# The last two projections taken apart into seven block products each, worked in pairs of batches

## The chip, the cores and the metric

One core of one Trainium2 chip runs the whole program. The time is device time in microseconds (us), the median of several executions. The program streams 128 batches through one long loop, so the steady turn of the loop, two ticks for four batches in the terms used below, repeated some 30 times, decides almost everything; the start and the drain are a few per cent.

## The reference, cut to what matters

```python
# layer 0: attention with a mask that multiplies the scores
h = jnp.maximum(_layernorm(x), 0.0)
q, k, v = (proj(Wq, bq), proj(Wk, bk), proj(Wv, bv))         # 512 x 512 each, 8 heads of 64
scores = einsum('bhqd,bhkd->bhqk', q, k) * SCALE * (adj + adj)[:, None]
ctx = einsum('bhqk,bhkd->bhqd', softmax(scores), v)
x = x + einsum('bse,fe->bsf', ctx, Wo) + bo                  # the output projection
# layer 1: graph attention
h = jnp.maximum(_layernorm(x), 0.0)
Wh = einsum('bsi,io->bso', h, W)                             # layer 1's projection
e = leaky_relu(Wh @ a[:512] + swapaxes(Wh @ a[512:], 1, 2), 0.2)
att = softmax(where(adj > 0.5, e, -9e15), axis=1)
x = x + elu(einsum('bst,bto->bso', att, Wh))
```

All is float32; x is 128 batches of 128 rows by 512 columns.

## The kernel before

The projections to q, k and v already use seven block products in place of eight (a "unit" below is one such product of a group of four batches: eight matmul instructions of 256 columns). The output projection and layer 1's projection are plain: four accumulating matmuls of 512 columns per batch, each into a PSUM tile of 512 columns, called a bank here.

```python
    def rows_matmul(lhsT, w):
        pm = ps1.tile([P, E], F32, name="pm", tag="ps1")
        for c in range(C):
            nc.tensor.matmul(pm, lhsT[:, c, :], w[:, c, :], start=(c == 0), stop=(c == C - 1))
        return pm

    def output0(b):
        po = rows_matmul(cxs[b], wo_sb)
        nc.vector.tensor_tensor(xs[b], po, xs[b], OP.add)
        l1s[b] = row_stats(xs[b])

    def hidden1(b):
        mv, rstd = l1s[b]
        h2 = work.tile([P, E], F32, name="h2", bufs=3)
        nc.vector.tensor_scalar(h2, xs[b], mv[:, 0:1], 0.0, op0=OP.subtract, op1=OP.max)
        # ... two dot products with u_src and u_dst on VectorE
        nc.vector.tensor_scalar(neg, adjTs[b], 0.5, NEG_INF, op0=OP.is_le, op1=OP.mult)

    def scores1(b):
        # ... broadcast transpose into pb, then
        nc.scalar.activation(w, pb, AF.Prelu, bias=ws[:, 1:2], alpha=ALPHA)
        nc.vector.tensor_tensor(w, w, neg, OP.add)
        nc.vector.tensor_reduce(nmx, w, AX.X, OP.max, negate=True)
```

One tick of its loop handles one batch t of attention, batch t-1 of the output projection and batch t-2 of layer 1 (the issue of loads, the drain and some helpers cut):

```python
            scores1(t - 2); softmax1(t - 2)
            scores(t); mask(t)
            done = unit(0); scale1(t - 2); done()
            exps(t); hidden(...); normalise(t)
            output0(t - 1)
            unit(1)()
            hidden1(t - 1)
            unit(2)()
            gather1(t - 2)
            done = unit(3); hidden(...); done()
            attn_T(t)
            unit(4)()
            stats0(far + 3); shift(t)
            output1(t - 2)
            unit(5)()
            context(t)
```

## Time and profile before

| | before |
|---|---|
| median time | 2660.1 us (2659.26 to 2661.6, 3 runs) |
| TensorE busy | 2615.8 us, 98% |
| VectorE / ScalarE busy | 1830 us, 69% / 1151 us, 43% |
| mean granted clock of TensorE | 0.997 |
| four batches in the steady loop | 81.14 us (40.57 a pair) |

TensorE is packed: instructions follow each other without gaps in the loop (2513.2 us busy of the 2521 between 79 and 2600 us), at full clock (1.00 in that stretch).

### The profile page before, as it was taken

What the parts mean: (1) busy time and instruction counts of PE and PEld (TensorE: products, weight loads), DVE (VectorE), ACT (ScalarE), POOL (GpSimd) and SP (SyncE); (2) the same over time, 40 slices, a digit from 0 to 9 for tenths busy, and PEclk for the clock granted to TensorE, in tenths of its full rate; (3) what the DMA queues carried; (4) which work ended last, traced back from release to release, by engine and by line L of the source; (5) the groups of instructions that cost most, each with busy time, mean ns of one, the idle gap of its engine ahead of it and who ended that gap; (6) DMA issues with size and microseconds to landing.
All of it is one profiled execution on the core that took longest, in us unless ns stands there. A gap on an engine that the chain in (4) does not pass through costs nothing.

```text
span 2655.8 us, 38303 instructions
## 1 busy us (share of the span) xinstructions
PE 2615.8 (98%) x13744; PEld 1882.8 (71%) x13744; DVE 1830.3 (69%) x3509; ACT 1151.3 (43%) x3595; POOL 334.7 (13%) x647
## 2 busy tenths in 40 slices
PE   7999999999999999999999999999999999999996
PEld 6677777777777777777777777777777777777763
DVE  5776767766676767677666767676776667676655
ACT  2444444444444444444444444444444444444443
POOL 1111111111111111111111111111111111111001
PEclk9999999999999999999999999999999999999999
DMA  4433322222321232222222223322222232122010
GB/s 153 68 74 70 64 64 64 65 64 66 77 56 57 74 70 64 64 65 63 64 67 77 58 54 75 69 64 64 66 62 64 67 77 58 55 75 57 31 40 20
DMA packets 209133, 173.29 MB, mean 65 GB/s; under 512 B 48432, under 2 KB 158000, under 8 KB 208560
## 3 DMA queue, kind: packets, MB, share of 16 engines
q1 hardware_dynamic: 207360, 170.84, 26.2%
q8 instruction: 109, 1.79, 0.4%
q14 instruction: 80, 0.66, 0.1%
q10 hardware_dynamic: 1584, 0.01, 0.0%
HBM read 137.11 MB, written 33.68 MB: 64 GB/s over the span
## 4 chain that ended last, share of the span: by engine, by line
PE 97%; DVE 2%; ACT 1%; DMA 1%; issue 0%; SPq 0%; ACTq 0%; DVEq 0%
PE pm L157 33%; PE acc_a L238 25%; PE acc_c L238 13%; PE acc_b L238 6%; PE sc L290 5%; PE pc L331 5%; PE pa L320 4%; PE pg L389 4%; PE pb L363 1%; ACT at L307 1%; DMA hT<-in_xT 0%; DVE at L314 0%; DVE nmx L300 0%; DVE at L296 0%; PE pt L177 0%; DMA x<-in_x 0%
## 5 line engine op out<-in xcount | busy, mean ns | idle before, releaser
L157 PE MATMUL pm<-w,gT 128*128 128x512 f32 x1024 | 464.0, 596 | 1.5 <-ACT gT L391 1.5
L157 PE MATMUL pm<-wo,cxT 128*128 128x512 f32 x1024 | 460.9, 593 | 0.5 <-ACT cxT L336 0.5
L307 ACT ACTIVATE at<-at,nmx 128x128 f32<-128x128 f32 x1024 | 395.6, 388 | 130.5 <-DVE nmx L300 130.5
L150 POOL TENSOR_SCALAR mv<-mv 128x1 f32<-128x1 f32 x256 | 117.1, 458 | 2149.8 <-DVE mv L147 2149.6
L157 PEld LDWEIGHTS pm<-w,gT 128*128 128x128 f32 x1024 | 195.4, 191 | 194.1 <-issue 185.9
L157 PEld LDWEIGHTS pm<-wo,cxT 128*128 128x128 f32 x1024 | 194.1, 190 | 191.1 <-issue 183.7
L399 DVE SCALAR_TENSOR_TENSOR x<-pm,x 128x512 f32<-128x512 f32 x128 | 88.5, 692 | 341.5 <-ACT ez L398 341.5
L398 ACT ACTIVATE ez<-pm 128x512 f32<-128x512 f32 x128 | 76.5, 598 | 399.2 <-PE pm L157 399.2
L238 PE MATMUL acc_a<-hT,wq 128*128 128x256 f32 x1024 | 246.7, 384 | 0.0
L238 PE MATMUL acc_a<-hT,wk 128*128 128x256 f32 x1024 | 245.3, 382 | 0.0
L238 PE MATMUL acc_a<-wv,hT 128*128 128x256 f32 x1024 | 244.2, 381 | 0.7 <-ACT v L250 0.7
L238 PEld LDWEIGHTS acc_a<-hT,wq 128*128 128x128 f32 x1024 | 190.7, 191 | 40.5 <-issue 14.8
L238 PEld LDWEIGHTS acc_a<-wv,hT 128*128 128x128 f32 x1024 | 189.4, 190 | 38.6 <-issue 14.8
L238 PEld LDWEIGHTS acc_a<-hT,wk 128*128 128x128 f32 x1024 | 187.2, 190 | 38.6 <-issue 14.8
L322 ACT COPY aT<-pa 128x1024 f32<-128x1024 f32 x128 | 129.6, 1012 | 147.4 <-PE pa L320 144.7
L307 ACT ACTIVATION_READ_ACCUMULATOR at<-at,nmx 128x1 f32 x1024 | 191.8, 187 | 0.0
L255 ACT ACTIVATE qT<-acc_a,bq 128x256 f32<-128x256 f32 x256 | 107.2, 470 | 194.6 <-PE acc_a L238 194.6
L145 DVE BATCH_NORM_STATS2 st<-x 128x6 f32<-128x512 f32 x256 | 176.4, 689 | 9.1 <-DMA x<-in_x 4.5
L151 POOL TENSOR_TENSOR mv<-mv,mhalf 128x1 f32<-128x1 f32 x256 | 177.3, 693 | 21.3
L331 PEld LDWEIGHTS pc<-aT,v 128*64 128x64 f32 x2048 | 109.2, 136 | 83.4 <-issue 83.4
L255 ACT ACTIVATE kT<-acc_a,bk 128x256 f32<-128x256 f32 x256 | 107.4, 471 | 134.0 <-PE acc_a L238 134.0
L314 DVE TENSOR_TENSOR at<-at,rs 128x1024 f32<-128x1024 f32 x128 | 156.8, 1225 | 4.4
(92 smaller groups left out, 3926.3 us busy)
## 6 DMA issues: line engine op xcount, KB each, us to landing
x<-in_x SPq DMA_DIRECT2D x256, 256.0 KB, 3.5
out<-x SPq DMA_DIRECT2D x128, 256.0 KB, 2.1
hT<-in_xT SPq DMA_DIRECT2D x120, 256.0 KB, 10.6
mr<-rows SPq DMA_DIRECT2D x120, 128.0 KB, 3.4
adj<-in_adj SPq DMA_DIRECT2D x128, 64.0 KB, 2.1
adjT<-in_adjT SPq DMA_DIRECT2D x128, 64.0 KB, 2.0
rows<-mv SPq DMA_DIRECT2D x120, 1.0 KB, 8.5
wq<-in_wqT SPq DMA_DIRECT2D x1, 1024.0 KB, 7.2
```

The lines of the kernel that those rows point to most:

```text
L145: nc.vector.bn_stats(st, src)
L150: nc.gpsimd.tensor_scalar_add(rstd, rstd, EPS)
L151: nc.gpsimd.tensor_tensor(rstd, rstd, mhalf, OP.pow)
L157: nc.tensor.matmul(pm, lhsT[:, c, :], w[:, c, :], start=(c == 0), stop=(c == C - 1))
L238: nc.tensor.matmul(acc[:, m, :], lhsT, rhs, start=fresh and m == 0 and c == 0, stop=c == 1, skip_group_check=True)
L255: nc.scalar.activation(dst(t, f)[:, m, :], a[:, m, :], AF.Identity, bias=bias[:, j : j + 1])
L290: nc.tensor.matmul(sc[:, s * C + i, :], qT[r, i, cols], kT[r, i, cols], start=True, stop=True)
L307: nc.scalar.activation(at[:, j, :], at[:, j, :], AF.Exp, bias=nmx[:, j : j + 1], accum_out=sums[:, j : j + 1])
L314: nc.vector.tensor_tensor(at, at, rs[:, :, None].to_broadcast([P, H, S]), OP.mult)
L320: nc.tensor.transpose(pa[:, j, :], at[:, j, :], ident)
L322: nc.scalar.copy(aT, pa)
L331: nc.tensor.matmul(pc[s * D : (s + 1) * D, i, :], vs[b // G][:, b % G, head * D : (head + 1) * D], ats[b][:, s * C + i, :], start=True, st ...
```

## The change

The intent is to take an eighth of the matmul work out of the last two projections too, by the scheme that q, k and v use already. Seven products of half-sized blocks need two batches as their two row blocks, so the pipeline goes by pairs: a tick is now a pair, with attention of batches a and b one after the other. VectorE gets the sums for the left factors and the adds of the products; to relieve it, layer 1's relu moves to ScalarE, and its mask is folded into one pass. The core of the diff, cut:

```diff
-    def rows_matmul(lhsT, w):
-        pm = ps1.tile([P, E], F32, name="pm", tag="ps1")
-        for c in range(C):
-            nc.tensor.matmul(pm, lhsT[:, c, :], w[:, c, :], start=(c == 0), stop=(c == C - 1))
-        return pm
+    PRODUCTS = [(0, 0, "a"), (1, 2, "b"), (5, 5, "a"), (6, 1, "c"), (4, 4, "a"), (2, 3, "a"), (3, 6, "c")]
+    def product_rows(left, w, which, n):
+        la, wb, bank = PRODUCTS[n]
+        slot = 1 if bank == "b" else 0
+        own = "c" if bank == "c" else "a"
+        if n == 0 or n == 3:
+            accs[which, own] = ps1.tile([P, 2, E // 2], F32, name="row_" + own, tag="ps1")
+        acc = accs[which, own][:, slot, :]
+        for c in range(2):
+            nc.tensor.matmul(
+                acc, left[:, la, c, :], w[:, wb, c, :], start=n in (0, 3) and c == 0, stop=c == 1, skip_group_check=True
+            )
+        return acc
     ... (output0: each product is added by VectorE as soon as it is there)
+        def done():
+            if n == 0 or n == 1:
+                add(0, 0, acc)
+            elif n == 2:
+                add(1, 0, acc)
     ...
-        nc.vector.tensor_scalar(h2, xs[b], mv[:, 0:1], 0.0, op0=OP.subtract, op1=OP.max)
+            nc.scalar.activation(h2[:, i, :], xs[p][:, i, :], AF.Relu, bias=nmr[:, i : i + 1], scale=mv[:, 1, i : i + 1])
     ...
+        nc.vector.scalar_tensor_tensor(w, adjTs.pop(p), 0.5, pb, op0=OP.is_le, op1=OP.subtract)
+        for i in range(2):
+            nc.scalar.activation(w[:, i, :], w[:, i, :], AF.Prelu, bias=ws[:, i, 1:2], scale=-MASK, alpha=ALPHA)
     ... (the tick, its first half; e is the pair in layer 1, o the one in the output projection, f the one that ends)
+            if attn:
+                scores(a)
+            if f is not None:
+                finish_a(f)
+            unit()()
+            if e is not None:
+                scores1(e)
+            if attn:
+                exps(a, range(4))
+            if e is not None:
+                softmax1(e)
+            if o is not None:
+                output0(o, 0)()
+            if attn:
+                exps(a, range(4, H))
+            if o is not None:
+                output0(o, 1)()
     ... (finish_b, a unit)
+            if e is not None:
+                scale1(e)
+            if attn:
+                normalise(a)
+            if o is not None:
+                output0(o, 2)()
     ... (unit, gather1, hidden, unit, attn_T(a), the first two products of output1, context(a), scores(b), ...)
     ... (the tick's end, its conditions cut: attn_T(b), hidden1(o), unit, output1(e, 5), then)
+            dots1(o, 0)
+            output1(e, 6)()
+            context(b)
+            dots1(o, 1)
+            elu(e)
+            context_sums()
```

Here o0, o1, o2 are the first products of `output0`; o0 and o1 take the two halves of one bank (`slot`). `scores(a)` also holds the VectorE work on the scores: the mask and its maximum.

## The prediction

> **What bounds the kernel now.** I read the page's busy shares first, then the chain that ended last, then the waits, then the timeline of one tick (one batch) in the steady part, then the stretches of the last 90 us.
>
> ```profile
> PE 2615.8 (98%) x13744; PEld 1882.8 (71%) x13744; DVE 1830.3 (69%) x3509; ACT 1151.3 (43%) x3595; POOL 334.7 (13%) x647
> PE 97%; DVE 2%; ACT 1%; DMA 1%; issue 0%; SPq 0%; ACTq 0%; DVEq 0%
> PE pm L157 33%; PE acc_a L238 25%; PE acc_c L238 13%; PE acc_b L238 6%; PE sc L290 5%; PE pc L331 5%; PE pa L320 4%; PE pg L389 4%; PE pb L363 1%; ACT at L307 1%; DMA hT<-in_xT 0%; DVE at L314 0%; DVE nmx L300 0%; DVE at L296 0%; PE pt L177 0%; DMA x<-in_x 0%
> ```
>
> TensorE is the chain (97%), and a third of it is pm, the output projection and layer 1's projection, the two that the change takes apart. A PE at 98% may still be loosely packed, so the starts matter more than the durations. From the chain in order of time, then the timeline of TensorE:
>
> ```profile
> 2453.30 3.45 PE acc_a L238 x16
> 2534.44 3.45 PE acc_a L238 x16
> ```
>
> ```profile
> 1212.81 3.60 PE L157 MATMUL pm<-wo,cxT 128*128 128x512 f32 x8
> 1216.24 1.89 PE L238 MATMUL acc_a<-hT,wq 128*128 128x256 f32 x8
> 1217.97 1.89 PE L238 MATMUL acc_b<-hT,wk 128*128 128x256 f32 x8
> 1219.69 1.05 PE L389 MATMUL pg<-w,h 128*128 128x128 f32 x8
> ```
>
> The same point of the loop returns after 81.14 us, for four batches: 40.57 us a pair. Eight instructions of 512 columns take 3.43 us from start to start, eight of 256 columns 1.73 us (0.216 each), so splitting columns costs nothing. No gap follows, because every input was ready long before. In this part VectorE and ScalarE never hold TensorE; the list of waits has TensorE waiting 18.3 us for normalised attention, six times, all at the end.
>
> The durations I need stand in the timeline of all engines, same tick:
>
> ```profile
> 1211.27 1.22 DVE L296 SCALAR_TENSOR_TENSOR at<-sc,adj 128x1024 f32<-128x1024 f32 x1
> 1212.52 1.22 DVE L300 TENSOR_REDUCE nmx<-at 128x8 f32<-128x1024 f32 x1
> 1213.65 0.15 DVE L380 RECIPROCAL rs<-sums 128x1 f32<-128x1 f32 x1
> 1213.77 0.40 ACT L307 ACTIVATE at<-at,nmx 128x128 f32<-128x128 f32 x1
> 1214.17 0.39 ACT L307 ACTIVATE at<-at,nmx 128x128 f32<-128x128 f32 x1
> 1222.32 1.04 PE L320 MATMUL pa<-ident,at 128*128 128x128 f32 x8
> 1223.39 1.01 ACT L322 COPY aT<-pa 128x1024 f32<-128x1024 f32 x1 [1.96 <-PE pa L320]
> ```
>
> A VectorE instruction of 1024 columns blocks the next for 1.25 us if that one needs its result, 1.13 if not. An exp of one head takes 0.39 us, four 1.55. ScalarE starts 0.2 us after TensorE has moved on.
>
> [...] The trace agrees: VectorE's order in the tick is the program's order. So one instruction that waits holds everything behind it. [...] The trace has 692 ns at 512 columns, 286 at 128[...]. So my estimate for the new 256-column operations is 0.42 us, blocking 0.45 or 0.34 us. [...] The trace, by stretches, after a wait of 3.0 us in the tail (columns from the second: length, PE, PEld, DVE, ACT, POOL, granted clock):
>
> ```profile
> 2603.00:2607.00 4.00, 0.97 (x9) 0.81 (x8) 1.69 (x3) 2.71 (x13) 0.00 (x0) 1.00 0.00 0
> 2607.00:2610.00 3.00, 3.00 (x11) 1.82 (x11) 2.83 (x7) 1.01 (x1) 1.50 (x2) 0.63 0.00 0
> 2610.00:2613.00 3.00, 3.00 (x6) 0.91 (x4) 1.02 (x4) 0.00 (x0) 0.62 (x1) 0.80 0.00 0
> ```
>
> It cost 1.7 us there (3 x 0.37 + 3 x 0.20), once in four waits of that length.
>
> **The change, part by part.** *TensorE work.* Removed per pair: 4 runs of pm, 4 x 3.43 = 13.72 us. Added: 14 products of 2 matmuls, each run as two instructions: 56 x 0.2156 = 12.07 us. Gain 1.65 us a pair, 38.9 us instead of 40.57; 64 x 1.65 = 106 us in all.
>
> *VectorE and ScalarE.* Added per pair: 8 sums of 256 columns for the left sides, 10 adds of 256 columns in place of 2 of 512. Removed: the relu of 0.48 x 2 (to ScalarE), the separate mask. Paired instructions save fixed cost. By the blocking times VectorE has some 32 us of work in 38.9. That is not a bound by itself, but it leaves little room for waits.
>
> *The order.* This is where I expect the change to lose. Take a tick (now a pair) with TensorE starting scores(a) at 0. TensorE's order is scores 1.15, projection unit 1.73, broadcast transposes 0.37, o0 and o1 (first two products of the output projection), so o1 would start at 0 + 1.15 + 1.73 + 0.37 + 0.86 = 4.1. But o0 and o1 are two halves of one PSUM bank, so o1 must wait until VectorE has added o0. In VectorE's order that add stands behind: the previous tick's last sums, mask(a) 1.25, its maximum 1.13, finish_a 1.13, the one-pass mask of layer 1 0.34, a round trip over ScalarE's Prelu 0.8, that maximum 0.35. With the add itself (0.45) this is 5.45 us after mask(a) starts.
>
> When does mask(a) start? At 1.35 at the earliest (scores ready). Before it VectorE must end the previous tick: attention's transpose ends at E-2.75 (E is the end of that tick's TensorE work: w5, w6 and context follow, 0.86 + 0.86 + 1.03), ScalarE copies it until E-1.55, only then comes the new relu (0.65, estimated from 598 ns for 512 columns plus a bias), so the first dot products start at E-0.9: dots 1.48, an add 0.35, dots 1.48, four sums 1.6: mask(a) at E+4.0. Where the previous tick is odd there is one more unit (1.73 us) behind the transpose; then the last dots end near E+1.35 and mask(a) is at E+2.9.
>
> So o0 is added at 2.9 + 5.45 = 8.4 (even ticks) and 4.05 + 5.45 = 9.5 (odd ticks), against 4.1: stalls of 4.3 and 5.4 us, mean 4.9. A second wait lies almost at the same depth in odd ticks: gather needs scale1, which stands behind q4's add, which waits for q4's copy on ScalarE behind all eight exps: 8.0 + 0.65 + 1.55 + 0.8 + 1.55 + 0.85 + 0.6 + 0.6 = 14.6; TensorE gets there at 9.3 + 5.4 = 14.7. It adds nothing once o1 has stalled, but would hold 5 us if o1 did not. The second half of the tick has slack: normalise(b) is due some 13 us after scores(b) and needs about 9.
>
> *Sum.* 38.9 + 4.9 = 43.8 us a pair, +3.2 on 40.57. For the 60 pairs of the full loop: +195 us. Clock: the idle stretches of 4.3 to 5.4 us exceed those that already dropped the clock; I take half the ticks at 1.2 us: +36. Start and tail: the first product waits behind sums of wv (some 3 us) and the last ticks are pair-long chains: +10. 2660 + 195 + 36 + 10 = 2901; I choose 2890.
>
> **Rivals.** (A) The stalls are hidden and TensorE stays packed: 2660 - 106 + 10 = about 2565. For it: the kernel before shows that such a schedule can be built. Against: even with mask(a) at 1.35, o0 is added at 6.8, 2.7 us late, and the gain is 1.65. (B) The compiler keeps the halves of the bank apart by address: o1 is free, and gather is the first wait, 1.9 us in even ticks (scale1 ends at 11.1 against 9.3) and 5.4 in odd ones: mean 3.6, (38.9 + 3.6 - 40.57) x 60 = +116, about 2790. (C) The previous tick's dots and sums overlap better than I think and mask(a) starts at 1.35 always: 2.7 us stall, +1.05 x 60 = +63, about 2735. (D) The clock drops in every tick: 2950. (E) VectorE becomes the bound: its 32 us plus waits of some 8 us would come near 43 anyway, so it can't be told from my own case by time alone; its busy share would be near 90%. (F) Transfers: the loads of the transposed x are issued a tick ahead and landed in 10.6 us; I expect none.
>
> **Range and chances.** C to D spans 2735 to 2950; with B between, I take 2740 to 2990 for 8 in 10. Faster needs both the bank wait and the tail chain to be wrong: 0.09. Within 2% (to 2713) needs stalls below 2.5 us a tick: 0.1. Slower: 0.81.
>
> **What would show it.** Right: TensorE's share falls to about 88 to 91%; the first in the list of TensorE's waits is the row accumulator on VectorE's add into x, 4 to 5 us some 60 times; VectorE 72 to 78%; granted clock below 9 tenths in some slices; the chain mixes DVE and ACT with PE. Wrong: PE still at 97% of the chain (A); waits chiefly at pg on w (B); a mask(a) that starts within 1.5 us of scores (C).

## The result and the profile after

| | before | after |
|---|---|---|
| median of the same rounds | 2659.95 us (4 runs, 2659.26 to 2661.6) | 3026.81 us (4 runs, 3026.47 to 3027.43) |
| TensorE busy | 2615.8 us | 2684.9 us |
| granted clock | 0.997 | 0.923 |
| four batches in the loop | 81.14 us | 92.16 us |

The change makes the kernel slower: ratio 1.1378, 95% interval 1.1359 to 1.1398. All ratios here are the mean time of one kernel's fast runs over the mean of the other's fast runs of the same rounds, so they are not quite the ratio of the medians quoted. The lower clock is in each of the four runs (0.923 or 0.924), so it belongs to the kernel.

From the page of the kernel after, busy time and then the chain that ended last, by engine and by line:

```profile
PE 2684.9 (89%) x15288; PEld 2265.9 (75%) x15288; DVE 2047.6 (68%) x3781; ACT 1301.2 (43%) x3915; POOL 119.1 (4%) x263
...
PE 73%; DVE 18%; issue 4%; ACT 4%; DMA 1%; POOL 0%; SPq 0%; POOLq 0%; DVEq 0%; ACTq 0%
PE acc_a L243 21%; PE row_a L295 17%; PE acc_c L243 9%; PE acc_b L243 7%; PE row_c L295 6%; DVE junk L407 6%; PE pg L445 4%; PE pa L334 4%; DVE at L312 3%; DVE x L490 3%; PE sc L310 2%; PE pc L354 2%; ACT w L421 1%; ACT aT L336 1%; DVE cxT L147 1%
```

Before, TensorE was 97% of the chain; now VectorE is 18% of it, by name the dot products (junk), the mask (at), the ending add (x L490) and the sums (cxT): instructions that stand ahead of o0's add. And TensorE is busy for longer than before with less to compute, which points to instructions that ran slower. The list of TensorE's waits (us in total, times, longest) begins with the one that was foretold:

```profile
PE row_a L295 <- DVE x L368: 296.4, 67, 8.7
```

In TensorE's timeline (start, length, instruction, instructions in the group; in brackets the recorded idle before it and who ended it) this is o0, o1 and the unit after them, in an even tick and then an odd one:

```profile
2539.41 1.03 PE L295 MATMUL row_a<-wo,cxT 128*128 128x256 f32 x4
2544.35 2.07 PE L295 MATMUL row_a<-wo,cxT 128*128 128x256 f32 x4 [3.91 <-DVE x L368]
2546.22 3.62 PE L243 MATMUL acc_b<-wv,hA 128*128 128x256 f32 x8
...
2584.69 1.03 PE L295 MATMUL row_a<-wo,cxT 128*128 128x256 f32 x4
2590.78 2.07 PE L295 MATMUL row_a<-wo,cxT 128*128 128x256 f32 x4 [5.06 <-DVE x L368]
2592.65 2.88 PE L243 MATMUL acc_a<-hS,wq 128*128 128x256 f32 x8
```

Two things are to be seen. First the wait: o1 stands 4.08 us behind where it could start in the even tick (2539.41 + 0.86 = 2540.27 to 2544.35), 5.23 us in the odd one. Second the lengths after it: o1 takes 2.07 us where o0, the same four instructions, took 1.03; the unit takes 3.62 or 2.88 instead of 1.89. The wait costs a second time, as clock.

What VectorE and ScalarE did in the odd tick's wait, from the timeline of all engines. TensorE's tick starts at 2581.55 with the scores of a:

```profile
2579.81 1.52 ACT L400 ACTIVATE h<-x,nmr,mv 128x512 f32<-128x512 f32 x2
2580.66 0.69 DVE L407 SCALAR_TENSOR_TENSOR junk<-h,u_src 128x512 f32<-128x512 f32 x1 [1.09 <-ACT h L400]
...
2583.69 0.42 DVE L146 TENSOR_TENSOR cxT<-cxT 128x256 f32<-128x256 f32 x1
...
2585.28 1.22 DVE L312 SCALAR_TENSOR_TENSOR at<-sc,adj 128x1024 f32<-128x1024 f32 x1
2586.53 1.22 DVE L316 TENSOR_REDUCE nmx<-at 128x8 f32<-128x1024 f32 x1
2587.67 1.22 DVE L490 SCALAR_TENSOR_TENSOR x<-z,x 128x1024 f32<-128x1024 f32 x1
2588.80 0.41 DVE L419 SCALAR_TENSOR_TENSOR w<-adjT,pb 128x256 f32<-128x256 f32 x1
2589.25 0.69 ACT L421 ACTIVATE w<-w,ws 128x128 f32<-128x128 f32 x2 [4.32 <-DVE w L419]
...
2590.31 0.41 DVE L368 TENSOR_TENSOR x<-row_a,x 128x256 f32<-128x256 f32 x1
```

The relu on ScalarE ends at 2581.33, 0.22 us before this tick begins, so most of the dot products and all sums of the previous pair run into this tick; the mask starts 3.73 us after the tick's start; and o0's add, the last line, ends 5.44 us after the mask started. o1 starts 0.06 us later. VectorE keeps the program's order here: o0 ends at 2585.72 (2584.69 + 1.03), but its add stays behind layer 1's maximum, which starts at 2589.98 after VectorE has sat idle for 0.76 us until ScalarE's Prelu is done.

The record of the granted clock changes in steps; I set the edges of the stretches on those steps (columns: stretch, length, PE, PEld, DVE, ACT, POOL, then granted clock, DMA share, GB/s):

```profile
2543.45:2550.28 6.83, 5.93 (x14) 4.71 (x15) 2.72 (x5) 3.91 (x21) 0.00 (x0) 0.50 0.19 74
...
2585.55:2587.82 2.27, 0.17 (x1) 0.00 (x0) 2.24 (x3) 0.00 (x0) 0.00 (x0) 1.00 0.00 0
2587.82:2594.65 6.83, 3.87 (x9) 3.12 (x10) 3.70 (x6) 4.54 (x22) 0.00 (x0) 0.50 0.00 1
```

The clock is halved for 6.83 us in either tick, and TensorE works for 5.93 and 3.87 us of it. Work at half clock takes twice as long (2.07 us for o1 against o0's 1.03), so half of that time is lost: (5.93 + 3.87) / 2 = 4.90 us in two ticks.

### The profile page after: what moved, and what is told of

Read it like the earlier page. It is cut to its first block, busy times and chain, and to the rows that moved or that the text cites. A ratio compares the mean times of both kernels' runs of the same rounds, so it can differ in the third digit from the quotient of the medians.

```text
span 3025.7 us, 40583 instructions
## 1 busy us (share of the span) xinstructions
PE 2684.9 (89%) x15288; PEld 2265.9 (75%) x15288; DVE 2047.6 (68%) x3781; ACT 1301.2 (43%) x3915; POOL 119.1 (4%) x263
## 3 DMA queue, kind: packets, MB, share of 16 engines
q8 instruction: 120, 1.97, 0.3%
## 4 chain that ended last, share of the span: by engine, by line
PE 73%; DVE 18%; issue 4%; ACT 4%; DMA 1%; POOL 0%; SPq 0%; POOLq 0%; DVEq 0%; ACTq 0%
PE acc_a L243 21%; PE row_a L295 17%; PE acc_c L243 9%; PE acc_b L243 7%; PE row_c L295 6%; DVE junk L407 6%; PE pg L445 4%; PE pa L334 4%; DVE at L312 3%; DVE x L490 3%; PE sc L310 2%; PE pc L354 2%; ACT w L421 1%; ACT aT L336 1%; DVE cxT L147 1%
## 5 line engine op out<-in xcount | busy, mean ns | idle before, releaser
L295 PE MATMUL row_a<-wo,cxT 128*128 128x256 f32 x1280 | 408.3, 449 | 296.7 <-DVE x L368 296.4
L295 PEld LDWEIGHTS row_a<-wo,cxT 128*128 128x128 f32 x1280 | 277.6, 227 | 366.0 <-DVE x L368 325.3
L295 PE MATMUL row_a<-w,gT 128*128 128x256 f32 x1280 | 330.2, 381 | 3.5 <-ACT z L466 1.9
L368 DVE TENSOR_TENSOR x<-row_a,x 128x256 f32<-128x256 f32 x320 | 134.5, 420 | 219.0 <-PE row_a L295 216.0
L295 PEld LDWEIGHTS row_a<-w,gT 128*128 128x128 f32 x1280 | 235.8, 191 | 34.2 <-ACT z L466 3.7
L312 DVE SCALAR_TENSOR_TENSOR at<-sc,adj 128x1024 f32<-128x1024 f32 x128 | 156.2, 1221 | 67.5 <-PE sc L310 67.5
L316 DVE TENSOR_REDUCE nmx<-at 128x8 f32<-128x1024 f32 x128 | 156.1, 1220 | 4.4
L243 PE MATMUL acc_a<-hS,wq 128*128 128x256 f32 x512 | 151.7, 450 | 0.0
L310 PE MATMUL sc<-kT,qT 64*128 64x128 f32 x2048 | 149.6, 286 | 0.0
L354 PE MATMUL pc<-aT,v 128*64 128x128 f32 x2048 | 141.0, 280 | 1.1 <-ACT aT L336 1.1
```

The lines of the kernel that those rows point to most:

```text
L243: nc.tensor.matmul(acc[:, m, :], lhsT, rhs, start=fresh and m == 0 and c == 0, stop=c == 1, skip_group_check=True)
L295: nc.tensor.matmul(acc, left[:, la, c, :], w[:, wb, c, :], start=n in (0, 3) and c == 0, stop=c == 1, skip_group_check=True)
L310: nc.tensor.matmul(sc[:, s * C + j, :], qT[r, j, cols], kT[r, j, cols], start=True, stop=True)
L312: nc.vector.scalar_tensor_tensor(at, sc, QSCALE, adjs[p][:, i : i + 1, :].to_broadcast([P, H, S]), op0=OP.mult, op1=OP.mult)
L316: nc.vector.tensor_reduce(nmx, at, AX.X, OP.max, negate=True)
L354: nc.tensor.matmul(pc[s * D : (s + 1) * D, j, :], vs[b // G][:, b % G, head * D : (head + 1) * D], aT[:, s * C + j, :], start=True, stop=True,
```

## The experiments

The theory has three parts. The bank: o1 waits only because it shares a bank with o0. The queue: the add that it waits for is late by VectorE's order, not by VectorE's load. The clock: each of these waits halves the clock for a while, which the prediction had put far too low. Rivals: VectorE is simply full (the prediction's E); and the halved clock is no effect of the waits, or costs only as much as predicted, and the rest is work in the loop that the sums missed. All seven kernels computed correct results. Six of them ran once; the kernel before took 2660.96 us (median of 7, from 2657.65 to 2664.73) beside the first four of them, 2662.61 and 2660.02 us beside the later ones. So runs of one kernel spread over some 7 us, and differences in total time that are read from single runs below are 66 us or more; the run with one useless matmul is read from the length of its turns instead.

### The second product in a bank of its own

```diff
-        slot = 1 if bank == "b" else 0
-        own = "c" if bank == "c" else "a"
-        if n == 0 or n == 3:
+        slot = 0
+        own = bank
+        if n == 0 or n == 1 or n == 3:
```

(and `start=n in (0, 1, 3)`.) It does so in both projections.

> The second product of each row projection gets a PSUM bank of its own. Mine: the changed kernel's wait at o1 (4.1 and 5.2 us in even and odd ticks) is one of the shared bank; with its own bank o1 runs at once, and TensorE waits later and in pieces: at o2 for the add of o0 (1.4 and 2.5 us), then in odd ticks at pg for w (2.4 us). Stalls 1.4 and 4.9 a tick, no piece over 3 us, so the clock seldom drops: 2740 to 2800 us, granted clock over 0.96. Rival (o1 waits for something else, such as the data of x or the queue): no change, 3010 to 3040.

Measured: 2809.38 us, clock 0.973, against 3026.81. The first two of TensorE's waits, and an odd tick:

```profile
PE row_a L295 <- DVE x L368: 131.7, 64, 5.6
PE pg L445 <- DVE rs L327: 27.9, 30, 2.3
```

```profile
2404.21 1.16 PE L295 MATMUL row_a<-wo,cxT 128*128 128x256 f32 x4 [2.47 <-DVE x L368]
```

The line is o2: it accumulates onto o0, so it has to wait for the same add, but one product and one unit (2.6 us) later. o1 no longer waits at all. The second line of the list is the gather's wait that rival B foresaw; it comes in odd ticks only, 0.9 us in the mean where B, which had no wait of o2 before it, had 5.4. So it was the sharing that held o1. The edit gives o1 a tile of its own and with it another place in PSUM, and which of the two the program's wait goes by, this run can't tell. The next waits in line are what the change would have cost without it: 2.47 us in odd ticks, 1.32 in even ones. The time lies 9 us above the expected range. The clock record says why: 33 spells of one window of 3.41 us each at half clock, of which TensorE works 3.30 us in the mean, 33 x 3.30 / 2 = 54 us. At full clock it would be some 2755 us, an estimate from that record.

### The ending add behind o0's add instead of ahead of it

```diff
-            if f is not None:
-                finish_a(f)
             unit()()
     ...
             if o is not None:
                 output0(o, 0)()
+            if f is not None:
+                finish_a(f)
```

> One VectorE instruction of 1.13 us (finish_a) goes from before the one-pass mask to after the add of o0; nothing else changes. Mine: the wait at o1 shrinks by 1.13 us in every tick (to about 3.0 and 4.1), 70 us in all, and the clock, which drops after long waits, gives back up to as much: 2870 to 2970. Rival (the wait is set by something not in VectorE's order): 3027 within 10 us.

Measured: 2919.36 us, clock 0.952. VectorE does exactly the same work, but o0's add comes one instruction of 1.13 us earlier; o1's recorded wait goes from 3.91 to 2.77 us and from 5.06 to 3.93:

```profile
2453.88 1.13 PE L295 MATMUL row_a<-wo,cxT 128*128 128x256 f32 x4 [2.77 <-DVE x L368]
```

```profile
2455.03:2458.44 3.41, 3.41 (x9) 2.67 (x9) 1.68 (x3) 1.86 (x10) 0.00 (x0) 0.50 0.26 100
```

Sixty ticks by 1.13 us are 68 us; the gain is 107 us. The rest is clock: 49 of its 65 low spells last one window of 3.41 us, where 61 of the changed kernel's 67 last two. Here the clock falls 1.15 us *after* o1 has started again. So a wait of 2.9 us (2450.94 to 2453.88) already halved the clock.

### Useless matmuls in the gap

```diff
             if o is not None:
                 output0(o, 0)()
+            if o is not None and attn:
+                idle = ps1.tile([P, 2, E // 2], F32, name="idle", tag="ps1")
+                for c in range(9):
+                    nc.tensor.matmul(idle[:, 0, :], ident, w1_sb[:, 0, 0, :], start=True, stop=True)
```

> Nine matmuls of no use (256 columns, 3.9 us) stand between o0 and o1, where TensorE would wait anyway. Mine: the wait for the add stays where it was in time, but the clock doesn't drop, and the products after it run at full speed: 2.7 us a tick less, about 2860 (2840 to 2890), granted clock at least 0.98. Rival (the slow products after the wait have another cause, such as the other engines' traffic, or the added work costs what it takes): 3027 or more, with the same slow products.

Measured: 2882.3 us, clock 0.993. More work and nothing else makes the kernel 144.5 us faster. The even tick:

```profile
2416.86 4.05 PE L610 MATMUL idle<-w,ident 128*128 128x256 f32 x18
2420.94 1.13 PE L295 MATMUL row_a<-wo,cxT 128*128 128x256 f32 x4
2421.91 1.89 PE L243 MATMUL acc_b<-wv,hA 128*128 128x256 f32 x8
```

o1 starts 8.08 us after the scores of a, to the hundredth what it is in the changed kernel (2536.27 to 2544.35): the dependence is untouched, so the products filled the gap without prolonging it. In odd ticks 1.18 us of the wait remain, and o1 starts 9.24 us after the scores against 9.23. But o1 and the unit run at full clock. This separates the two costs: two ticks take 87.37 us, so work and waits are 43.69 us a pair, and the clock is 92.16 - 87.37 = 4.79 us in two ticks, beside the 4.90 read from the clock record.

### The same work in another order

The first half of the tick, everything else as in the changed kernel (a bank shared, relu on ScalarE, the same instructions in number and shape):

```diff
             if attn:
                 scores(a)
-            if f is not None:
-                finish_a(f)
+            unit()()
+            unit()()
             unit()()
             if e is not None:
                 scores1(e)
+            if o is not None:
+                output0(o, 0)()
+            if e is not None:
+                softmax1(e)
             if attn:
                 exps(a, range(4))
+            done = unit()
             if e is not None:
-                softmax1(e)
-            if o is not None:
-                output0(o, 0)()
+                scale1(e)
+            if f is not None:
+                finish_a(f)
             if attn:
                 exps(a, range(4, H))
+            done()
     ... (output0(o, 1); gather1 and the later units moved likewise, no unit added in all)
```

> The same work with the first half of the tick in another order: three projection units before o0, o0's add ahead of finish_a, layer 1's softmax ahead of the exps, one unit between o0 and o1, one ahead of attention's transpose. Mine: TensorE waits for nothing in the loop, a pair takes 38.9 to 39.5 us, 2560 to 2610 us in all, granted clock 0.99. Rival (VectorE with its 32 us of work and its waits is a bound of its own near 43 us a pair): 2800 or more, VectorE over 75% busy.

Measured with three rounds: 2597.47 us (2595.63 to 2598.26), ratio to the kernel before 0.9763, interval 0.9747 to 0.978: faster than both. From its page:

```profile
PE 2529.9 (98%) x15288; PEld 2165.9 (84%) x15288; DVE 2043.3 (79%) x3781; ACT 1288.1 (50%) x3915; POOL 119.4 (5%) x263
...
PE 86%; ACT 8%; DVE 4%; DMA 1%; issue 1%; POOL 0%; SPq 0%; POOLq 0%; DVEq 0%; ACTq 0%
```

VectorE has the same 3781 instructions and 2043 us of work as in the changed kernel and ends 429 us sooner. So it was never full, and the rival E falls. The three units between the scores and o0, 5.2 us of TensorE work that depends on none of this, cover the time in which VectorE catches up. The run moves several things at once (the units, o0's add, finish_a, the scaling of layer 1); how much each is worth, it doesn't show. Two ticks take 78.23 us, 39.12 us a pair (2206.59 to 2284.83 between the scores of a): TensorE's own work but for a recorded wait of 0.16 us in every second tick, predicted as 38.9.

### A little more work per tick: does the loop lock to the clock?

In the changed kernel two ticks take 92.16 us in every turn. The clock record of this kernel changes in steps of one length: its low spells last 3.41, 6.83 or 10.24 us (but for the last, which the end cuts off), the drops in the loop are 44.37 and 47.79 us apart in turn, and all of these are whole multiples of 3.4133 us (in ns, 6827 / 2 and 10240 / 3). In the kernel before, the first two drops, at 64.83 and 2607.76 us, are 745.00 such lengths apart. A window below is one such length: the low spells in the loop of the changed kernel last 6.83 us (two windows), in other kernels here also 3.41, the drops are 13 and 14 windows apart in turn, and 92.16 / 3.4133 = 27.00. If the loop is locked to the windows, a little more work should vanish (theory L); if 27.00 is chance, it should add up (theory N). First one useless matmul, 0.43 us a tick, behind `context(a)`:

```diff
+                idle = ps1.tile([P, 2, E // 2], F32, name="idle", tag="ps1")
+                nc.tensor.matmul(idle[:, 0, :], ident, w1_sb[:, 0, 0, :], start=True, stop=True)
```

> The changed kernel with one useless matmul of 256 columns (0.43 us of TensorE) a tick, in the stretch after the wait where TensorE sets the pace. In the changed kernel two ticks last 92.16 us, 27.00 times the 3.413 us[...], in every turn of the loop; in the other runs the ratio is no whole number. Theory L (the loop has locked on the clock's windows: added work moves the next wait within its window and the clock gives less back): the period stays 92.16 or jumps to another whole number of windows; total within 8 us of 3027, or a jump of more than 60. Theory N (the whole number is chance): two ticks 93.0 us, total 3027 + 64 x 0.43 = 3054, within 8.

Measured: 3030.6 us. The first gather of layer 1, two ticks apart:

```profile
2506.14 1.95 PE L445 MATMUL pg<-w,h 128*128 128x128 f32 x16
...
2598.31 1.95 PE L445 MATMUL pg<-w,h 128*128 128x128 f32 x16
```

That is 92.17 us again: 0.86 us of work per two ticks was added, and the turn kept its length. 30 of its low spells now last one window and 31 two, so the clock gave back what the work took. Then three useless matmuls at the same place, 1.29 us a tick:

> Three useless matmuls a tick (1.29 us of TensorE) where the run before had one. Theory L (the loop is locked on the clock's windows): two ticks stay at 92.16 us, or go to the next whole number of windows, 95.57; total 3027 to 3037, or about 3135. Theory N (no lock; the one matmul was hidden by chance): 92.16 + 2.59 = 94.75 us, total about 3110.

Measured: 3128.28 us. The same point of the loop:

```profile
2544.27 1.95 PE L445 MATMUL pg<-w,h 128*128 128x128 f32 x16
...
2639.85 1.95 PE L445 MATMUL pg<-w,h 128*128 128x128 f32 x16
```

95.58 us are 28.00 windows, where adding up would give 92.16 + 2 x 1.29 = 94.74. 59 of the gaps from drop to drop are 14 windows, two are 13. The total lies 18 us above what adding up was expected to give, and 7 below the 3135 of the jump. The settling itself can be seen: two ticks from the scores of tick 2, 4 and 6 (counted from 0) take 94.78, 95.45 and 95.54 us before the turn stays at 95.57, and 93.19, 92.27 and 92.19 before 92.16 with one useless matmul. The lock is shown by both runs for this order of work. Other orders here have no such lock: two ticks take 25.92 windows (88.47 us) with the later add and 24.91 (85.04 us) with the bank of its own in most turns. How a turn comes to settle at a whole number, no run shows.

### Layer 1's relu back on VectorE

The relu becomes one `tensor_scalar` per batch on VectorE, as before the change; the scale of the rows moves into two small factors, one on GpSimd and one on VectorE (edit cut):

```diff
-            nc.scalar.activation(h2[:, i, :], xs[p][:, i, :], AF.Relu, bias=nmr[:, i : i + 1], scale=mv[:, 1, i : i + 1])
+            nc.vector.tensor_scalar(h2[:, i, :], xs[p][:, i, :], mv[:, 0, i : i + 1], 0.0, op0=OP.subtract, op1=OP.max)
```

> One part of the change undone: layer 1's relu is on VectorE again (0.48 us each, as before the change, its scale folded into the scores and the softmax), all else as changed. Mine: in ticks after an even one the dot products no longer stand behind the copy of attention's transpose on ScalarE, so mask(a) starts some 1.1 us earlier and the wait at o1 falls from 5.2 to about 4.1 us; in the others the last unit's add holds the dots and nothing moves. 31 x 1.1 = 34 us less, the clock may add or take some 30: 2960 to 3020. Rival (the relu's place doesn't matter, VectorE has only more to do): 3027 to 3060.

Measured: 2961.25 us, clock 0.945. VectorE has 128 instructions more and is busy for 50 us more, and the kernel is 66 us faster: the dot products need not wait for ScalarE's copy of attention and its relu. o1's recorded wait in odd ticks falls from 5.06 to 3.75 us; in even ticks, which follow a tick with a unit more behind the transpose, it goes from 3.91 to 3.97. Over 30 turns that is some 38 us of waits (30 x 1.25); the rest of the 66 is clock. So in this order of work the relief of VectorE hurt, by lengthening the chain into the next tick. It makes up a quarter of the odd ticks' wait, (5.06 - 3.75) / 5.06, and is not the main cause.

### When does a wait halve the clock?

No new kernel, but a count over the traces of seven of these (all but the kernel before and the reordered one): each of TensorE's recorded waits over 1 us, from 150 us after the start on, is laid over the 3.413 us windows, whose edges the drops give, and the largest idle time that falls into a single window is compared with whether the clock fell.

```
largest idle in one window   waits   clock fell after
under 1.9 us                    79      4
1.9 to 2.0 us                   22     11
2.0 us and more                314    314
```

(The times are rounded to 0.01 us; a recount may move one or two waits over a bound. The four of the first line are short waits in the drain, with a long wait after each in the same window.) So in these kernels it is not the length of a wait that counts but how much of one window it leaves idle: about 2 us, well under the 3.413 us of a whole one. For the waits of these seven kernels that means: under 1.9 us a wait is nearly always free (no drop after 75 of the 79 with under 1.9 us in a window), and from about 4 us on it cannot be split so that both windows stay under 2. In between, the position decides: waits of 3.75 us (relu on VectorE, odd ticks) halved the clock 20 times out of 29, of 3.93 us (later add, odd ticks) 28 times out of 30, and in all eleven exceptions the window's edge cut the wait into two parts of 1.98 us or less. The waits of the changed kernel, 3.91 and 5.06 us as recorded, halve the clock in every one of their 59 occurrences in the steady loop; 2.77 us in the kernel with the later add did so 29 times out of 29; 2.25 to 2.5 us in the one with its own bank 30 times out of 35; 1.32 us there not once in 29.

## Why the prediction was right or wrong

The direction and the mechanism were right; the time, 3026.8 us, lies above the predicted range of 2740 to 2990. Step by step:

| per pair or in all | predicted | measured |
|---|---|---|
| TensorE's work, a pair | 38.9 us | 39.12 us (reordered kernel) |
| wait of o1, even / odd tick | 4.3 / 5.4 us | 4.08 / 5.23 us |
| mask starts after the last tick's end, even / odd | 2.9 / 4.05 us | 2.58 / 3.73 us |
| from mask's start to o0's add done | 5.45 us | 5.44 us |
| work and waits, a pair | 43.8 us, +195 in all | 43.69 us, (43.69 - 40.57) x 60 = +187 in all |
| clock | +36 us | 4.79 x 30 = +144 us |
| start and drain | +10 us | +36 us |
| sum over the kernel before | +241 (chose +230) | +367 us |

*The matmul work.* Right in the main: the seven products save 1.45 us a pair where 1.65 was predicted, but only a packed order shows it.

*The bank.* Right, and shown by the kernel with a bank of its own, whose o1 waits no more. That o1 must wait was the assumption, which no trace of the kernel before shows; in the changed kernel o1 starts 0.06 us after the end of o0's add. Rival B (halves of a bank kept apart by address) falls with it. The price here is 4.08 us in even ticks and 5.23 in odd ones; with a bank of its own the kernel takes 217 us less (3026.81 - 2809.38), of which a part is clock.

*VectorE's order.* Right to about 0.3 us in each part. The chain from the mask to o0's add was worked out as 5.45 us and took 5.44. VectorE's new adds of 256 columns (L368 on row_a), estimated at 0.42 us from 692 ns at 512 columns and 286 at 128, took 420 ns in the mean of 320. Rivals A (hidden) and C (the mask starts early) fall by the wait list and by the mask's start; F (transfers) has no part in it, for the list of TensorE's waits has no transfer in it. A was right about what the schedule could be: the reordered kernel, at 2597 us, comes near to its 2565.

*The clock.* This is the step that failed: "I take half the ticks at 1.2 us: +36". Both factors were too small. Each tick drops the clock, not half of them, and a drop costs 2.4 us, not 1.2: the kernel before shows a spell of one window in its tail, and the prediction took something less than that (a second spell near the end, from 2641.89 us, lasts two windows after a wait of 3.88 us, with 5.72 us of work in it; the prediction didn't look at it), while the long waits here halve the clock for two windows, of which 5.93 and 3.87 us are work. Measured in two ways, 4.79 and 4.90 us per two ticks, it is 144 us instead of 36, so 108 of the 137 us between the prediction's 2890 and the result. Rival D had the drop in every tick, but at some 1.4 us a drop by its total of 2950 (85 us over 60 ticks, worked back from 2660 + 195 + 10); at the prediction's 1.2 us it would be 2937. The prediction counted one example in four, and scaled that; it should have asked whether a wait that comes in every turn can be an occasional cost. Its own trace could have told it more: laid on windows of 3.413 us whose edges the one drop gives, the four waits of 2.98 to 3.02 us in the tail of the kernel before leave at most 1.97, 1.78, 2.54 and 1.58 us of one window idle, and only the one with 2.54 dropped the clock. That agrees with the count above, in a kernel that the count left out; a wait of 4.3 or 5.4 us can't be placed so that it stays under 2 us in every window.

*Start and drain.* Mis-sized too: 36 us for 10. The turns of the loop give 60 x (46.08 - 40.57) = 331 of the 367 us; 36 are left. The traces show where most is: the first scores start at 56.8 us instead of 51.9, and from the start of the last scores to the end it is 67 us instead of 41.5, probably because the three ticks that drain the pipeline now hold a pair each. The reordered kernel, with next to no waits, has this too: its loop gains 60 x 1.45 = 87 us and the kernel 63. No run took the ends apart, so which part of them is needed stays open.

*The signs.* TensorE's share fell to 89% as foretold, the wait list began with the row accumulator (67 times, 4.4 us in the mean), the chain mixed the engines. VectorE's share came out at 68% instead of 72 to 78%, mostly because the span was longer (over the predicted 2890 us its 2047.6 us would be 71%). The slices of the page showed the clock too coarsely, at 9 tenths nearly throughout; its stretches by steps were needed.

## What to carry to other kernels

When a change splits work so that a result is handed to another engine several times a turn, work out when the *first* hand-over is served in that engine's order, and put independent work of the waiting engine in front of it: the same instructions took 3027 us in one order and 2597 in another. Where TensorE must wait in every turn of a loop, count the clock for every turn, half of the work done in the one or two windows after it (here 4.79 us in two ticks), and don't trust small edits near such a wait: here the turn once swallowed 0.86 us of added work and once jumped by a whole window. An engine that is only two thirds busy (VectorE, 68%) can still be the one that sets the time, and relieving it by a longer chain made that worse here (3027 us against 2961).
